# Four-head softmax tiles with a separate mask and maximum, re-timed planner costs, and a shorter warm-up in a one-core attention and feed-forward block

## The chip, the cores and the metric

The kernel runs on one core of a Trainium2 chip. The metric is device time in microseconds (us) of one execution; lower is better. The core has TensorE (PE, matrix products; its weight loads are PEld), VectorE (DVE), ScalarE (ACT), GpSimd (POOL) and SyncE (SP, which here only issues DMA transfers).

## What is computed

A layer of a transformer in float32, with the normalisation after each half. The input has 2 sequences of 1024 rows and 512 columns; attention has 16 heads of 32 columns and a causal mask; the feed-forward part uses the signs of its weights.

```python
qkv = jnp.einsum('bsd,ed->bse', x, w_qkv) + b_qkv          # 16 heads of 32
scores = jnp.einsum('bhqd,bhkd->bhqk', q, k) / math.sqrt(Hd)
scores = scores + causal[None, None]                       # -inf above the diagonal
out = jnp.einsum('bhqk,bhkd->bhqd', softmax(scores), v)
x = layernorm(x + jnp.einsum('bsd,ed->bse', out, w_out) + b_out)
hidden = relu(jnp.einsum('bsd,hd->bsh', x, sign(up_weight)) * up_scale)   # 2048 wide
out = jnp.einsum('bsh,dh->bsd', hidden, sign(down_weight)) * down_scale * output_scale
x = layernorm(x + out)
```

## The kernel before

The attention is done in eight chunks, two sequences by four groups of four heads. For each chunk the kernel makes queries, keys and values (`project`: products L554 for queries and keys, L591 for values), splits queries and keys into a rounded part and a remainder (`split`, `split_keys`), and lets SyncE copy them into the `stacks` tiles (`stack`), so that one pass of the float32r matmul gives a nearly exact score. Then it goes over row blocks of 128 queries, i = 0 to 7, each with (i + 1) x 128 keys.

A score tile ("sc", the program's `d`) is one of two PSUM buffers of 1024 columns. `grouped` puts four heads into a tile for i below 2, two for i below 4, else one. For a tile (`scores`): the score matmuls (L839; L820 for the first four row blocks of the first chunk, which use plain float32 and at most two heads), then one VectorE pass per head that adds the mask, negates and takes the minimum, which is minus the maximum (L857), then one ScalarE exponential per head with the row sum (L872), a reciprocal (L884), and a scaling per head on GpSimd (L890). TensorE transposes the result (L911, `transposes`), four 128x128 blocks to a PSUM bank, VectorE or ScalarE copies the bank to SBUF (L492 to L494), and TensorE multiplies with the values (L940, `values`). The output projection (L1005, `output`), the normalisation (`normalise`, which raises to the power -0.5 on GpSimd), the turned input (L1073), and the feed-forward products (L1122 and L1159) follow.

Nothing is issued in the order in which it is written. Each piece is a task with an engine, or a choice of engines, a cost, a due place and the tiles that it reads and writes. `Plan.schedule` runs a list scheduler over all tasks with these costs, chooses engines and buffers, and the instructions are issued in the order that comes out. The costs (`mm`, `dve`, `act`, `pool`, `copy` and the pairs given in braces) therefore do no work on the chip; they decide the order on every engine and which engine makes a copy. In a pair the first number is how long the engine is held, the second when the result is there.

The first stage (`first_half`) is ordered mostly by hand: 24 transposes of the identity (L710) on TensorE as a warm-up, then the first key and query weights on ScalarE's DMA queue, the first 256 columns of the transposed input in four pieces and the next 256 in one on SyncE's, then the products for these columns (L754) and their biases (L771 on VectorE for queries, L779 on ScalarE for keys). The bias vector `bqk` is loaded by GpSimd ahead of everything (L336). Five copies of one column (`hold`, L701) make later transfers wait for the first input piece.

Of the kernel before, what the change touches and what calls it, by code (L numbers as in the profile page):

```python
# [13 lines left out]
ALU = mybir.AluOpType  # L14
# [4 lines left out]
P = 128  # L19
# [257 lines left out]
def kernel(  # L277
# [55 lines left out]
    half = const.tile([P, 1], F32, tag="half", name="half")  # L333
    nc.gpsimd.memset(half, -0.5)
    bqk = const.tile([P, b_qkvP.shape[1]], F32, tag="bqk", name="bqk")
    nc.gpsimd.dma_start(bqk, b_qkvP)  # L336
    ups = const.tile([P, NFC], F32, tag="ups", name="ups")
    osc = const.tile([P, 1], F32, tag="osc", name="osc")
    bo = const.tile([P, D], F32, tag="bo", name="bo")
# [27 lines left out]
    def place_for(stack, name, n, kind=F32, side="left"):  # L367
# [24 lines left out]
        "v": views(a_v, (NQ, P)),  # L392
        "wout": views(a_wo, (NC, D)),
        "xb": views(a_xb, (D,)),
        "atT": views(a_at, (NC, P)),
        "nm": views(a_sm, (NU,))[:NSM],
        "sums": views(a_sm, (NU,), at=NSM * NU)[:NSM],
# [67 lines left out]


    def mm(n):
        return {"PE": (max(0.112, n / 2400 + 0.018),) * 2}

    def fp32(n):  # L470
        return {"PE": (n / 600 + 0.009,) * 2}
# [31 lines left out]
    def new(cls, after=(), blocks=1):  # L503
        t = plan.tile(cls, [y for c in after for y in all_of[c]], blocks)
        all_of[cls].append(t)
        return t

    def dma(place, dst, src, kb, reads=(), writes=(), updates=(), queue=DMA, label="dma", after=()):
        def fn(e):
            engine[e].dma_start(dst(), src())  # L510

        return plan.task(
            queue, fn, place, reads, writes, updates, size=kb, label=label, after=after
        )
# [190 lines left out]
    def first_half():  # L705

        warm = new("f")
        for k in range(24):
            plan.task(
                TURN, lambda _, k=k: nc.tensor.transpose(of(warm)[:, k % 4, :], ident, ident), -300,  # L710
                updates=[warm[0]], label="warm",
            )
        act_queue = {"ACT": (0.5, 0.5)}
        w = weights[0, 0] = new("w")
        for c, z in ((0, 1), (1, NC)):
            dma(
                -100,
                lambda c=c, z=z: of(w)[:, c:z, 1, :],
                lambda c=c, z=z: w_qkvT[c * P : z * P, D : D + P].rearrange(
                    "(c p) f -> p c f", p=P  # L720
                ),
                64 * (z - c),
                writes=[w[1, k] for k in range(c, z)],
                queue=act_queue,
            )
        xt = inputs[0] = new("xT")
        for t0, pieces in ((0, NC), (HB, 1)):
            for c in range(0, NC, NC // pieces):
                z = c + NC // pieces
                dma(  # L730
                    -100,
                    lambda c=c, z=z, t0=t0: of(xt)[:, c:z, t0 : t0 + HB],
                    lambda c=c, z=z, t0=t0: xT[c * P : z * P, t0 : t0 + HB].rearrange(
                        "(c p) t -> p c t", p=P
                    ),
                    128 * (z - c),
                    updates=[xt[k, t0] for k in range(c, z)],
                )
        load_w(0, 0, -95, [0], act_queue)
        hold(  # L740
            lambda: of(xt)[:, 0, 0:1], [xt[0, 0]],
            [lambda: of(w)[:, 0, 2, 0:1], *[lambda c=c: of(xt)[:, c, TB : TB + 1] for c in range(NC)]],
            [w[2], *[xt[c, TB] for c in range(NC)]],
        )
        load_w(0, 0, -90, [2])
        load_x(0, -80, [TB])
        v, kq = new("v"), new("pt", blocks=8)
        rows = lambda n: of(kq)[:, n * TB : (n + 1) * TB]
        for t0 in (0, HB):
            for n in (1, 0):  # L750
                ps = new("f")
                for c in range(NC):
                    def fn(_, c=c, n=n, t0=t0, ps=ps):
                        nc.tensor.matmul(  # L754
                            bank(ps)[:, :HB],
                            lhsT=of(w)[:, c, n, :],
                            rhs=of(xt)[:, c, t0 : t0 + HB],
                            start=(c == 0),
                            stop=(c == NC - 1),
                        )  # L760

                    plan.task(
                        fp32(HB), fn, -50, [xt[c, t0], w[n, c] if n else w[n]],
                        updates=[ps[0]], count=2, label="ps",
                    )
                bias = bqk[:, n * NC : n * NC + 1]
                dst = lambda n=n, t0=t0: rows(n)[:, t0 : t0 + HB]
                if n == 0:
                    plan.task(
                        dve(0.42),  # L770
                        lambda _, dst=dst, ps=ps, bias=bias: nc.vector.tensor_scalar(  # L771
                            dst(), bank(ps)[:, :HB], bias, scale, ALU.add, ALU.mult
                        ),
                        -50, [ps[0]], [kq[n, t0]], label="bias",
                    )
                else:
                    plan.task(
                        act(0.47),
                        lambda _, dst=dst, ps=ps, bias=bias: nc.scalar.activation(  # L779
                            dst(), bank(ps)[:, :HB], AF.Identity, bias=bias  # L780
                        ),
                        -50, [ps[0]], [kq[n, t0]], label="bias",
                    )
        values_of(0, 0, v, 0, lambda units=0: -1)
        plain[0, 0] = kq, v
# [25 lines left out]
    def scores(b, e, i, heads, at):  # L811
# [38 lines left out]
                        updates=[sc[0]], label="sc",  # L850
                    )

        for j in range(G):
            some = lambda j=j: of(sc)[:, j * W : j * W + N]
            plan.task(
                dve(0.17 + 1.046 * N / 1000),
                lambda _, j=j, some=some: nc.vector.tensor_tensor_reduce(  # L857
                    some(),
                    some(),
                    mask[:, S - N :],  # L860
                    scale=-1.0,
                    scalar=LARGEST,
                    op0=ALU.add,
                    op1=ALU.min,
                    accum_out=of(nm)[:, j : j + 1],
                ),
                at, [sc[0]], [sc[1, j], nm[j]], label="max",
            )
        for j in range(G):
            plan.task(  # L870
                {"ACT": (0.355 + 0.838 * N / 1000, 0.46 + 0.838 * N / 1000)},
                lambda _, j=j: nc.scalar.activation(  # L872
                    of(pr)[:, j * N : (j + 1) * N],
                    of(sc)[:, j * W : j * W + N],
                    AF.Exp,
                    bias=of(nm)[:, j : j + 1],
                    scale=-1.0,
                    accum_out=of(sums)[:, j : j + 1],
                ),
                at, [sc[1, j], nm[j]], [pr[j], sums[0]], label="exp",  # L880
            )
# [46 lines left out]
    def values(b, e, some, at):  # L928


        for i, _ in some:
            if (b, i) not in atT:
                atT[b, i] = new("atT")
        to, v = new("po"), (made.get((b, e)) or plain[b, e])[1]

        def fn(_):
            for n, (i, each) in enumerate(some):
                for k in range(i, -1, -1):
                    for u, pt, c in each[::-1]:
                        nc.tensor.matmul(  # L940
                            of(to)[ts(u, HD), n, :],
                            lhsT=of(v)[:, k, ts(u, HD)],
                            rhs=of(pt)[:, ts(c + k, P)],
                            start=(k == i),
                            stop=(k == 0),
                        )

        blocks = sum(i + 1 for i, _ in some)
        last = max(i for i, _ in some)
        plan.task(  # L950
            {"PE": (0.28 + 0.218 * blocks, 0.2 + 0.218 * blocks)}, fn, at,
            [v[t] for t in range(0, (last + 1) * P, TB)]
            + [pt[0] for _, each in some for _, pt, _ in each],
            updates=[to[0]], count=8 * blocks, label="po",
        )
        for n, (i, _) in enumerate(some):
            rows = atT[b, i]
            plan.task(
                dve(0.345),
                lambda _, n=n, rows=rows: nc.vector.tensor_scalar(  # L960
                    of(rows)[:, e, :],
                    of(to)[:, n, :],
                    bqk[:, 2 * NC + e : 2 * NC + e + 1],
                    None,
                    ALU.add,
                ),
                at - FAST, [to[0]], [rows[e]], label="at",
            )
# [59 lines left out]
    def normalise(b, at):  # L1028
# [7 lines left out]
            at, [m[0]], [m[1]], label="eps",  # L1036
        )
        plan.task(
            pool(1.2),
            lambda _: nc.gpsimd.tensor_tensor(  # L1040
                rs(), rs(), half.to_broadcast([P, NQ]), ALU.pow
            ),
# [298 lines left out]
```

## Time and profile before

| | us |
|---|---|
| median of three runs | 776.39 (776.19 to 776.39) |
| profiled execution | 775.87 |
| its span, first to last instruction | 774.1 |
| TensorE busy / weight loads | 756.1 / 574.9 |
| VectorE, ScalarE, GpSimd busy | 492.4, 368.9, 259.1 |
| attention part ends, feed-forward runs to the end | near 505 |

The span is what the trace covers; the execution's time has 1.8 us around it. In lines of the timeline the columns are start, duration, engine and line, operation, and in brackets how long the engine sat idle before it and what ended that. In stretches there is, for each engine, busy time and the number of instructions. In groups by shape, the numbers after the first bar are busy time in all and the mean duration in ns; after the second bar, the idle time before. A matmul in float32 is two instructions; the recorded durations of matmuls overlap, so the pitch from start to start is what TensorE is held for.

### The profile page before, as it was taken

The page shows a single profiled execution, that of the slowest core. Times are in us where ns is not written, and L with a number is a line of the kernel's source. Part 1 is how long each engine was busy: PE and PEld are TensorE (multiplying, and loading weights), DVE is VectorE, ACT ScalarE, POOL GpSimd, SP SyncE. Part 2 cuts the span into 40 slices and gives each one's busy share as a digit, 9 for nine tenths or more (in the row PEclk, how much of TensorE's full clock was granted, in tenths as well). Part 3 has the DMA queues.
Part 4 walks back from the last instruction along what each step waited for, and adds up shares of the span by engine and source line. Part 5 has one row for each costly group of instructions (what it writes and reads, how often), then busy time and mean ns, then how long its engine had stood idle before and what let it go on. Part 6 is the DMA issues. An engine that isn't in the chain of part 4 may idle for free.

```text
span 774.1 us, 15524 instructions
## 1 busy us (share of the span) xinstructions
PE 756.1 (98%) x5880; PEld 574.9 (74%) x5880; DVE 492.4 (64%) x1258; ACT 368.9 (48%) x823; POOL 259.1 (33%) x329
## 2 busy tenths in 40 slices
PE   8999999999999999999999999999999999999996
PEld 6668768768756776886876877657787787878884
DVE  2557878778766676877777878855337337335535
ACT  2337665666744455666666567744222222222210
POOL 3316445445535444544544545431002002002000
PEclk9999999999999999999999999999999999999999
DMA  5476436146453423523604614333001001000101
GB/s 163 106 175 148 135 83 140 40 100 155 130 110 83 96 69 85 111 67 68 152 1 95 139 56 137 137 109 109 1 0 55 1 0 55 1 0 1 55 0 54
DMA packets 38617, 62.35 MB, mean 81 GB/s; under 512 B 6032, under 2 KB 19344, under 8 KB 38544
## 3 DMA queue, kind: packets, MB, share of 16 engines
q1 hardware_dynamic: 37440, 60.85, 30.6%
q8 instruction: 46, 0.75, 0.4%
q10 hardware_dynamic: 1072, 0.52, 0.2%
q14 instruction: 27, 0.22, 0.1%
q0 software_dynamic: 32, 0.01, 0.0%
HBM read 24.66 MB, written 4.19 MB: 37 GB/s over the span
## 4 chain that ended last, share of the span: by engine, by line
PE 86%; DVE 9%; ACT 3%; issue 1%; POOL 1%; ACTq 0%; POOLq 0%; DVEq 0%
PE s L1122 14%; PE pd L1159 14%; PE s L911 13%; PE s L554 12%; PE d L839 9%; PE s L940 9%; PE s L1005 6%; PE s L591 6%; DVE d L857 3%; ACT probs L872 2%; DVE probsT L494 1%; PE s L754 1%; ACT probsT L492 1%; DVE small L1189 1%; PE s L1073 1%
## 5 line engine op out<-in xcount | busy, mean ns | idle before, releaser
L890 POOL TENSOR_SCALAR probs<-probs,small 128x128 f32<-128x128 f32 (+7 forms) x256 | 188.6, 748 | 249.6 <-DVE small L884 231.0
L872 ACT ACTIVATE probs<-d,small 128x128 f32<-128x128 f32 (+7 forms) x256 | 189.1, 748 | 61.6 <-DVE small L857 33.9
L857 DVE CUSTOM_DVE_ANT_0 d<-d,mask 128x128 f32<-128x128 f32 (+7 forms) x256 | 194.0, 765 | 31.5 <-PE d L839 19.9
L911 PE MATMUL s<-ident,probs 128*128 128x128 f32 x1152 | 164.4, 273 | 1.7 <-DVE probsT L494 0.8
L911 PEld LDWEIGHTS s<-ident,probs 128*128 128x128 f32 x1152 | 133.9, 141 | 32.8 <-issue 19.9
L492 ACT COPY probsT<-s 128x512 f32<-128x512 f32 (+3 forms) x184 | 90.9, 528 | 129.4 <-PE s L911 114.8
L1159 PE MATMUL pd<-stacks,hid 128*128 128x512 f32 x512 | 133.1, 399 | 0.5 <-DVE hid L1139 0.5
L1122 PE MATMUL s<-xt,stacks 128*128 128x512 f32 x512 | 132.7, 399 | 0.0
L1133 ACT ACTIVATE hf<-s,ups 128x512 f32<-128x512 f32 x64 | 44.0, 688 | 164.1 <-PE s L1122 162.4
L554 PE MATMUL s<-xT,wqkv 128*128 128x512 f32 x240 | 119.0, 599 | 2.1 <-ACT probsT L492 1.6
L839 PE MATMUL d<-stacks 128*128 128x512 f32 (+2 forms) x368 | 117.0, 416 | 1.1 <-ACT probs L872 0.4
L1159 PEld LDWEIGHTS pd<-stacks,hid 128*128 128x128 f32 x512 | 94.1, 188 | 24.2 <-DVE hid L1139 1.4
L1122 PEld LDWEIGHTS s<-xt,stacks 128*128 128x128 f32 x512 | 94.3, 188 | 23.4 <-issue 1.0
L494 DVE COPY probsT<-s 128x512 f32<-128x512 f32 (+3 forms) x161 | 91.1, 582 | 27.4 <-PE s L911 24.4
L1139 DVE CAST hid<-hf 128x512 fp32r<-128x512 f32 x64 | 27.3, 427 | 121.5 <-ACT hf L1133 121.4
L839 PEld LDWEIGHTS d<-stacks 128*128 128x128 f32 x368 | 58.7, 190 | 37.5 <-issue 20.4
L940 PEld LDWEIGHTS s<-probsT,v 128*32 128x32 f32 x2304 | 60.4, 110 | 20.4 <-ACT probs L872 7.6
L591 PE MATMUL s<-wqkv,xT 128*128 128x128 f32 x512 | 73.3, 275 | 0.0
L940 PE MATMUL s<-probsT,v 128*32 128x128 f32 x2304 | 71.6, 274 | 1.4 <-ACT probsT L492 1.0
L591 PEld LDWEIGHTS s<-wqkv,xT 128*128 128x128 f32 x512 | 67.2, 191 | 6.2 <-issue 4.8
L1005 PE MATMUL s<-wout,atT 128*128 128x512 f32 x128 | 63.7, 595 | 0.5 <-ACT probsT L492 0.5
L554 PEld LDWEIGHTS s<-xT,wqkv 128*128 128x128 f32 x240 | 39.2, 190 | 25.2 <-issue 20.6
(66 smaller groups left out, 496.1 us busy)
## 6 DMA issues: line engine op xcount, KB each, us to landing
stacks<-wqkv SPq DMA_DIRECT2D x224, 128.0 KB, 2.4
wqkv<-in_w_qkvT SPq DMA_DIRECT2D x22, 256.0 KB, 3.7
rows<-in_x SPq DMA_DIRECT2D x16, 256.0 KB, 2.7
raw<-in_up_wT SPq DMA_DIRECT2D x4, 1024.0 KB, 5.0
out<-atT SPq DMA_DIRECT2D x16, 256.0 KB, 2.0
xT<-in_xT SPq DMA_DIRECT2D x12, 256.0 KB, 5.5
stacks<-wqkv SPq DMA_DIRECT2D x48, 64.0 KB, 2.0
raw<-in_down_wT SPq DMA_DIRECT2D x2, 1024.0 KB, 5.5
```

The costliest lines, as they stand in the source:

```text
L494: nc.vector.tensor_copy(dst, src)
L554: nc.tensor.matmul(of(ps).rearrange("p a b -> p (a b)"), lhsT=of(w)[:, c, n, :], rhs=of(xt)[:, c, t0 : t0 + TB], start=(c == 0), stop=(c = ...
L591: nc.tensor.matmul(of(ps)[:, t, :], lhsT=of(xt)[:, c, t0 + t * P : t0 + (t + 1) * P], rhs=of(w)[:, c, 2, :], start=(c == 0), stop=(c == NC ...
L839: nc.tensor.matmul(of(sc)[:, j * W + k0 : j * W + k1], lhsT=of(st)[:, 0, u, ts(i, P)], rhs=of(st)[:, 1, u, k0:k1], start=True, stop=True,)
L857: lambda _, j=j, some=some: nc.vector.tensor_tensor_reduce(some(), some(), mask[:, S - N :], scale=-1.0, scalar=LARGEST, op0=ALU.add, op1= ...
L872: lambda _, j=j: nc.scalar.activation(of(pr)[:, j * N : (j + 1) * N], of(sc)[:, j * W : j * W + N], AF.Exp, bias=of(nm)[:, j : j + 1], sca ...
L890: lambda _, j=j: nc.gpsimd.tensor_scalar(of(pr)[:, j * N : (j + 1) * N], of(pr)[:, j * N : (j + 1) * N], of(sums)[:, j : j + 1], 1.0, ALU. ...
L911: lambda _, k=k, c=c, tp=tp: nc.tensor.transpose(of(tp)[:, k, :], of(pr)[:, c], ident),
L940: nc.tensor.matmul(of(to)[ts(u, HD), n, :], lhsT=of(v)[:, k, ts(u, HD)], rhs=of(pt)[:, ts(c + k, P)], start=(k == i), stop=(k == 0),)
L1005: lambda _, c=c: nc.tensor.matmul(bank(py), lhsT=of(a)[:, c, :], rhs=of(wout)[:, c, :], start=(c == 0), stop=(c == NC - 1),),
L1122: lambda _, f=f, c=c, n=n, pu=pu: nc.tensor.matmul(of(pu), lhsT=of(up)[:, f // TPB, c, ts(f % TPB, P)], rhs=of(xt)[:, n, c, :], start=(c = ...
L1159: lambda _, f=f, t=t, n=n, h=h: nc.tensor.matmul(of(pds[t]), lhsT=of(h)[:, ts(t, P)], rhs=of(dn)[:, f // 4, f % 4, :], start=(f == 0 and n ...
```

## The change

There are five edits.

1. Tiles of four heads: the four fused passes become one add of the mask's last 128 columns to the last 128 columns of each head, and one reduction that gives the negated maximum of all four heads. The exponential then runs with scale +1, not -1. Tiles of one and two heads stay as they are.
2. Costs of the plan: the least cost of a float32r matmul 0.062 (was 0.112), the exponential held 0.25 + 0.852 N/1000 (was 0.355 + 0.838 N/1000), the value group 0.15 + 0.218 per block (was 0.28), the power on GpSimd 1.7 (was 1.2), and costs for the two new operations.
3. The bias vector is no longer loaded by GpSimd; it is a tile of the plan, loaded on ScalarE's queue between the first key weights and the rest of them. The two first biases now depend on it in the plan.
4. The first input columns come in three pieces (one, one and two blocks of rows), not four.
5. Twelve warm-up transposes, not 24.

```diff
-    nc.gpsimd.dma_start(bqk, b_qkvP)
...
-        return {"PE": (max(0.112, n / 2400 + 0.018),) * 2}
+        return {"PE": (max(0.062, n / 2400 + 0.018),) * 2}
...
-        for k in range(24):
+        for k in range(12):
...
+            if c == 0:
+                dma(-100, lambda: bqk, lambda: b_qkvP, 8, writes=[biases[0]], queue=act_queue)
...
-        for t0, pieces in ((0, NC), (HB, 1)):
-            for c in range(0, NC, NC // pieces):
-                z = c + NC // pieces
+        for t0, c, z in ((0, 0, 1), (0, 1, 2), (0, 2, NC), (HB, 0, NC)):
...
-                        -50, [ps[0]], [kq[n, t0]], label="bias",
+                        -50, [ps[0], biases[0]], [kq[n, t0]], label="bias",
...
+        sign = 1.0 if G == 4 else -1.0
+        if G == 4:
+            sc3 = lambda: of(sc).rearrange("p (g w) -> p g w", g=G)[:, :, :N]
+            plan.task(
+                dve(0.163 + 0.134 * G),
+                lambda _: nc.vector.tensor_tensor(
+                    sc3()[:, :, N - P :],
+                    sc3()[:, :, N - P :],
+                    mask[:, None, S - P :].to_broadcast([P, G, P]),
+                    ALU.add,
+                ),
+                at, [sc[0]], [sc[1, j] for j in range(G)], label="mask",
+            )
+            plan.task(
+                dve(0.15 + 1.046 * N * G / 1000),
+                lambda _: nc.vector.tensor_reduce(of(nm)[:, :G], sc3(), AX.X, ALU.max, negate=True),
+                at, [sc[1, j] for j in range(G)], [nm[j] for j in range(G)], label="max",
+            )
...
-                {"ACT": (0.355 + 0.838 * N / 1000, 0.46 + 0.838 * N / 1000)},
+                {"ACT": (0.25 + 0.852 * N / 1000, 0.37 + 0.852 * N / 1000)},
...
-                    scale=-1.0,
+                    scale=sign,
...
-            {"PE": (0.28 + 0.218 * blocks, 0.2 + 0.218 * blocks)}, fn, at,
+            {"PE": (0.15 + 0.218 * blocks, 0.21 + 0.218 * blocks)}, fn, at,
...
-            pool(1.2),
+            pool(1.7),
```

## The prediction

> **What bounds the kernel now.** I read the page's busy times first, then the busy time by stretch, then the timeline of the first 25 us, then the waits of TensorE's weight loads, then the groups by shape. The page and the stretches:
>
> ```profile
> PE 756.1 (98%) x5880; PEld 574.9 (74%) x5880; DVE 492.4 (64%) x1258; ACT 368.9 (48%) x823; POOL 259.1 (33%) x329
> 0.00:10.00 10.00, 7.79 (x38) 7.46 (x39) 0.40 (x5) 1.28 (x1) 2.62 (x11) 1.00 0.84 254
> ...
> 750.00:775.00 25.00, 16.36 (x71) 12.84 (x69) 12.95 (x28) 2.55 (x6) 1.50 (x1) 0.93 0.11 42
> ```
>
> TensorE is the bound. It lacks 774.1 - 756.1 = 18.0 us: 2.2 before its first instruction, 24.1 - 16.4 = 7.7 after its last, and 8.1 in between. So work off TensorE is worth nothing unless TensorE waits for it, and three things can move the time: when real matmuls start, how the new order makes TensorE wait, and the tail. The start, from the timeline:
>
> ```profile
> 2.21 5.08 PE L710 MATMUL s<-ident 128*128 128x128 f32 x24 [2.21 <-POOL ident masks.py:199]
> ...
> 7.13 3.62 PE L754 MATMUL s<-xT,wqkv 128*128 128x256 f32 x16
> 8.02 1.28 ACT L779 ACT_TABLE_LOAD   x1 [8.02 <-DMA bqk<-in_b_qkvP]
> 10.35 0.47 ACT L779 ACTIVATE probsT<-s,bqk 128x256 f32<-128x256 f32 x1 [1.05 <-PE s L754]
> 10.79 0.48 DVE L771 TENSOR_SCALAR probsT<-s,bqk 128x256 f32<-128x256 f32 x1 [6.90 <-PE s L754]
> ...
> 11.42 0.50 PE L820 MATMUL d<-probsT 32*128 32x128 f32 x8 [0.67 <-DVE probsT L771]
> ```
>
> The 24 warm-up transposes fill TensorE from 2.21 to 7.13, one every 212 ns. The 16 instructions of the first key and query products follow, one every 216 ns. The first scores wait 0.67 us for the query bias on VectorE. The key bias waits for its product, not for the bias vector (landed at 8.02).
>
> **What the skill says.** The Trainium skill, "TensorE: Matmul & The Clock Gate", Part 1 (The HAM clock gate), says that TensorE runs at half rate until it has been busy for about 3.4 us. The trace agrees: a warm-up transpose takes 212 ns from start to start, while eight later ones (L911 at 149.58) take 1.03 us less one 0.27 us tail, 109 ns each. The same page (Engine queue depths) says that VectorE and ScalarE are strictly first in, first out, so a late head holds up what is behind; the 0.67 us wait above is of that kind. "DMA: Bandwidth & Descriptors", SWDGE vs HWDGE vs iDMA, says that transfers issued from ScalarE and SyncE run on the same DMA engines and have faster setup than GpSimd's. Here GpSimd's 6 KB bias took 5.5 us to land, ScalarE's 64 KB took 2.9. The first half is not contradicted: the DMA engines are 0.84 busy in the first 10 us.
>
> **The change, part by part.**
>
> *Start.* Twelve warm-ups go: 12 x 0.212 = 2.54 us of TensorE filler. The real gain ends where the data is. In the trace the first input block (issued 0.73, 2.7 us to land) is there at 3.4 and the first key weights (0.72 + 2.9) at 3.6. The rest of the key weights were issued at about 1.2 and landed 4.1 later, at 5.3; the last of the four input blocks (2.1 + 4.8) at 6.9, the query weights (1.65 + 4.9) at 6.6. New: ScalarE issues four transfers at 0.48 us each (1.43 us for three now), the bias second, so the key and query weights start 0.48 later: about 5.8 and 7.1. Input blocks 2 and 3 become one transfer of the same bytes; I put it between the old 5.7 (block 2) and 6.9 (block 3), at 6.7. The order of the changed program also puts all of the key product ahead of the query product, where now they alternate. So: transposes to 2.21 + 12 x 0.212 = 4.75; key block 0 at half rate, 2 x 0.43, to 5.6; block 1 from 5.8 to 6.65; blocks 2 and 3 from 6.7, 4 x 0.216, to 7.6; query 8 x 0.216, to 9.3. Now the query product ends at 10.75. Gain 1.4 us. Key bias and its table load come off the path altogether; the query bias still costs its wait. Bounds: 2.5 (all warm-ups count) and 0 (the clock wakes a window later and eight instructions take 0.43 instead of 0.216, which costs 1.7).
>
> What hangs on it moves too. GpSimd does the key cast (L616) now at 14.99 after three normalisations, in the new order after two; SyncE's chain of 48 stack transfers begins right behind it at 15.61, one per 0.63 us, and supplies the first scores of L839 at 50.23. It should begin some 2 us earlier, the scores that need it come some 2.3 us earlier: no new wait there, within 0.5 us. GpSimd loses a 0.77 us issue at 2.43, where it idles until 13.96; ScalarE gains a 0.48 us issue, where it idles until 8.02. SyncE issues one transfer less. All nothing.
>
> *Four heads per step.* These are the first two row blocks of seven of the eight chunks, 14 tiles (the reciprocal on 128x4 counts 14). From the groups by shape:
>
> ```profile
> L857 DVE CUSTOM_DVE_ANT_0 d<-d,mask 128x1024 f32<-128x1024 f32 x32 | 38.9, 1232 | 1.3 <-PE d L839 0.9
> ...
> L857 DVE CUSTOM_DVE_ANT_0 d<-d,mask 128x256 f32<-128x256 f32 x32 | 13.8, 431 | 7.6 <-ACT probs L872 3.7 <-PE d L839 2.7 <-PE d L820 0.8
> ...
> L857 DVE CUSTOM_DVE_ANT_0 d<-d,mask 128x128 f32<-128x128 f32 x32 | 9.5, 300 | 3.0 <-PE d L839 1.5 <-PE d L820 0.8
> ...
> L1020 DVE BATCH_NORM_STATS2 small<-x 128x6 f32<-128x512 f32 x8 | 5.5, 692 | 0.1
> L1016 DVE TENSOR_TENSOR x<-s,rows 128x512 f32<-128x512 f32 x8 | 5.5, 690 | 4.7 <-PE s L1005 4.7
> ```
>
> Now four passes and their four accumulator reads start 0.43 us apart at 128 columns and 0.52 at 256 (timeline, 12.06 to 18.46): 1.72 and 2.08 us a tile. New: one add over 4x128 (like L1016, 0.69) and one reduction over 512 (like L1020, 0.69) or 1024 elements (like the 1232 ns pass): 1.38 and 1.92. VectorE saves 7 x (0.34 + 0.16) = 3.5 of 492.4 us. Nothing of it is on the path by itself. Against it, the first exponential waits for the whole pair, not for one pass: 1.38 - 0.43 = 0.95 and 1.92 - 0.52 = 1.4 us later, and the score buffer is released after four exponentials (0.36 and 0.47 each, 0.2 for the last read): at 3.0 and 4.0 us instead of 2.3 and 2.7. There are two such buffers. Pricing the matmuls in the changed program's order by their pitch, TensorE has at least 4.5 us of other work before it needs one back after such a tile, mostly 4.5 to 6.9. Cover holds with 0.5 to 2.9 us to spare for a queue on VectorE. I take 0; bounds -1 (VectorE's relief) to +5 (14 x 0.35).
>
> *The plan's costs.* They do no work; they change the order. On TensorE the order stays alike over most of the attention part and is the same from about 505 us on, the tail included. Where it differs I look at the wait that matters:
>
> ```profile
> PEld d L839 <- ACT probs L872: 14.9, 39, 1.0
> PEld s L940 <- ACT probs L872: 7.6, 10, 0.8
> ```
>
> These are loads of score and value matmuls held until a score buffer or a copied block is free; most are hidden behind running matmuls. In the new order the first 640-column tile's buffer is wanted again after one short value group and two matmuls, 1.2 us, where its maximum, exponential (0.83 + 0.14 + 0.81) and semaphores need about 2.1: +0.9 us, once, near 48 us. In the old order that gap is 2.3 or more. The last long value group of the attention part follows its last transposes by 0.2 us, not 0.65, with a copy of 0.69 between: +0.4. On the other side, the exponential is now planned at its real pitch (0.25 + 0.852 x 0.256 = 0.47 us at 256 columns, the 0.47 of the timeline; the old plan had 0.57), and a 128-column matmul at 0.07 instead of 0.112: copies move three blocks from VectorE to ScalarE. I credit 0.8 of the 8.1 us idle in between; bounds -3 to +4. Sum: +0.5.
>
> **Sum.** -1.4 + 0 + 0.5 = -0.9 us on the profiled execution of 775.87 (its span 774.1 and 1.8 around it). The median of the runs, 776.39, is 0.5 above it; on that, 775.4.
>
> **Rivals.** A measurement can tell 0.2%, 1.55 us, from no change.
> - *Start gain kept, partly given back in the new order*: 775.4, within the bound. For it: a gain that the arrival of data limits, two places that lose by count. I give it 0.35.
> - *The clock wakes late*: with fewer warm-ups and a wait for data, the first products run at half rate, -1.4 + 1.7 + 0.5 = +0.8: 777.2. Against it: TensorE has next to no pause between 2.2 and 6.7. 0.08.
> - *The order gains as well*: an exponential planned right keeps ScalarE's queue true, and TensorE loses 1.5 us less of its 8.1: -1.4 - 1.5 = -2.9, 773.5. For it: VectorE is 75 to 80% busy in the attention stretches (38 of 50 us), so its relief may count. 0.38.
> - *Slower: the score buffers*. The pair of the four-head tiles holds a buffer 0.7 and 1.3 us longer. Where VectorE has a copy of 0.69 us ahead of the pair, release moves to 4.7, past the 4.5 us of cover; it decides from there. At 0.35 us for each of 14 tiles, 4.9 - 1.4 + 0.5 = +4.0: 780.4; half as many tiles, 777.9. Against it: the plan knows this hold. 0.19.
>
> **How the numbers follow.** Faster 0.38; within 0.2% 0.35 + 0.08 = 0.43; slower 0.19. The time is the likeliest case's, 775.4; that case alone spans 774.3 to 776.8. The range takes in most of the faster and about half of the slower case: 772.6 to 778.6.
>
> **What would show it.** Right: the last of the first 16 product instructions starts near 9.1, not 10.5; the first stack transfer near 13.5; L839's first scores near 48, with a wait of about 1 us behind them; VectorE some 3 to 4 us less busy; the part after 505 us unchanged but shifted. Wrong: first products at 430 ns each until 9 or 10 (late clock); a new wait of score matmuls on the exponentials of 128x128 and 128x256 tiles (buffers); idle time of TensorE in between well below 8 or above 10 us (the order).

## The result, and the profile after

| | before | after |
|---|---|---|
| median of six runs each, us | 775.91 | 772.87 |
| lowest to highest | 775.13 to 776.39 | 772.42 to 773.81 |
| ratio, with its 95% interval | | 0.9963 (0.9950 to 0.9976) |
| span of the profiled execution | 774.1 | 771.3 |
| first scores (L820 / L821) start | 11.42 | 13.14 |
| first feed-forward product (L1122 / L1143) starts | 520.77 | 518.04 |

The changed kernel is faster by 0.37%, 3.0 us, more than the 0.2% that can be told from no change. The forecast was 775.4 with a range from 772.6 to 778.6, its likeliest case no change beyond 0.2%: the range holds the time just above its low end, and what came is the case to which it gave 0.38, by other steps than its own. That the range holds is luck: two terms were wrong by 3.1 and by 4.95 us, with opposite signs.

Three stretches take the span apart. To the first scores the new kernel is 13.14 - 11.42 = 1.7 us slower. From there to the first feed-forward product it needs 504.9 us, not 509.35: 4.45 us faster. From there to the end it is 253.3 us in both. So the start lost where a gain was forecast, and the attention part gained where a small loss was.

The middle stretch, before and after, in the columns of the stretches (length, then busy time and instructions of TensorE, its weight loads, VectorE, ScalarE and GpSimd; the share of the clock, the DMA engines' busy share and GB/s):

```profile
11.42:520.77 509.35, 502.45 (x4767) 371.66 (x4767) 372.94 (x1015) 306.70 (x726) 238.38 (x305) 1.00 0.42 104
```

```profile
13.14:518.04 504.90, 500.13 (x4766) 372.37 (x4767) 373.69 (x929) 306.74 (x726) 238.07 (x305) 1.00 0.42 104
```

TensorE's idle time falls from 6.9 to 4.8 us, so 2.1 of the 4.45 us come out of idle time. The other 2.3 come out of its busy time, with the same matmuls: so recorded busy time is not all work, and what shortens in it no view shows.

The page of the changed kernel, busy times; then its timeline at the start (start, duration, engine, what, and the idle time before with what ended it):

```profile
PE 754.0 (98%) x5868; PEld 574.7 (75%) x5868; DVE 494.2 (64%) x1174; ACT 368.9 (48%) x823; POOL 257.7 (33%) x328
```

```profile
2.19 2.82 PE L710 MATMUL s<-ident 128*128 128x128 f32 x12 [2.19 <-POOL ident masks.py:199]
...
4.11 1.28 ACT L780 ACT_TABLE_LOAD   x1 [4.11 <-DMA bqk<-in_b_qkvP]
...
4.81 1.06 PE L755 MATMUL s<-xT,wqkv 128*128 128x256 f32 x2
...
7.33 5.14 PE L755 MATMUL s<-xT,wqkv 128*128 128x256 f32 x14 [1.45 <-DMA wqkv<-in_w_qkvT]
10.26 0.47 ACT L780 ACTIVATE probsT<-s,bqk 128x256 f32<-128x256 f32 x1 [4.87 <-PE s L755]
12.51 0.48 DVE L772 TENSOR_SCALAR probsT<-s,bqk 128x256 f32<-128x256 f32 x1 [8.67 <-PE s L755]
...
13.14 0.49 PE L821 MATMUL d<-probsT 32*128 32x128 f32 x4 [0.67 <-DVE probsT L772]
```

The transposes now end near 4.8 and the first key block runs there, as forecast. Then TensorE stands for 1.45 us until the rest of the key weights is there, and the fourteen instructions from 7.33 take 5.14 us, 0.37 each, where the kernel before needed 0.216: they start 0.43 us apart up to 10.9, at half rate, and 0.216 apart from there. The bias is early (table load at 4.11), the weights are late. The DMA issues of the first 2.6 us say so; the columns are the transfer, the issuing queue, count, size, and us from issue to landing. Before:

```profile
wqkv<-in_w_qkvT ACTq DMA_DIRECT2D x1, 256.0 KB, 4.9
wqkv<-in_w_qkvT ACTq DMA_DIRECT2D x1, 192.0 KB, 4.1
```

After:

```profile
wqkv<-in_w_qkvT ACTq DMA_DIRECT2D x1, 256.0 KB, 7.1
wqkv<-in_w_qkvT ACTq DMA_DIRECT2D x1, 192.0 KB, 5.6
wqkv<-in_w_qkvT ACTq DMA_DIRECT2D x1, 64.0 KB, 2.9
bqk<-in_b_qkvP ACTq DMA_DIRECT2D x1, 6.0 KB, 2.9
```

The same two weight transfers, behind the 6 KB of the bias, need 2.2 and 1.5 us longer from their own issue.

In the attention part, these are the waits of the weight loads in the changed kernel, and TensorE's own (us in all, times, longest):

```profile
PEld d L840 <- ACT probs L893: 22.6, 58, 0.9
...
PEld s L961 <- ACT probs L893: 7.6, 10, 0.8
```

```profile
PE d L840 <- ACT probs L893: 2.6, 4, 0.7
PE s L710 <- POOL ident masks.py:199: 2.2, 1, 2.2
PE s L932 <- DVE probsT L494: 1.7, 2, 0.9
PE s L755 <- DMA wqkv<-in_w_qkvT: 1.5, 1, 1.5
```

The wait for score buffers has grown, from 14.9 us to 22.6, while the part became faster: this sum alone doesn't explain the gain. Where it lies shows in one chunk. The timeline of before, near the group of 64 value matmuls of the second chunk:

```profile
145.71 1.12 PE L554 MATMUL s<-xT,wqkv 128*128 128x512 f32 x2 [0.53 <-ACT probsT L492]
...
146.76 1.69 PEld L940 LDWEIGHTS s<-probsT,v 128*32 128x32 f32 x64 [0.76 <-ACT probs L872]
...
152.46 0.30 PEld L839 LDWEIGHTS d<-stacks 128*128 128x128 f32 x2 [0.95 <-ACT probs L872]
```

and of after, in the same chunk:

```profile
150.79 1.28 DVE L494 COPY probsT<-s 128x512 f32<-128x512 f32 x2
...
152.38 0.68 DVE L878 CUSTOM_DVE_ANT_0 d<-d,mask 128x512 f32<-128x512 f32 x1
...
155.44 0.30 PEld L840 LDWEIGHTS d<-stacks 128*128 128x128 f32 x2 [0.94 <-ACT probs L893]
155.44 0.56 PE L840 MATMUL d<-stacks 128*128 128x512 f32 x2 [0.71 <-ACT probs L893]
```

The product that waited 0.53 us for a copy behind exponentials no longer waits; in exchange two copies now stand ahead of a maximum on VectorE (150.79, then 152.38), and the score buffer that it releases comes 0.71 us late. The gain is the sum of such differences, chunk after chunk. TensorE is 1.7 us behind the kernel before at the first scores, 0.3 ahead at the last value product of the third chunk, 2.1 at that of the fifth and 2.7 at the first feed-forward product; no single wait carries it.

### The profile page after: what moved, and what is told of

It is laid out like the page before. It is cut to its first block, busy times and chain, and to the rows that moved or that the text cites. A ratio compares the mean times of both kernels' runs of the same rounds, so it can differ in the third digit from the quotient of the medians.

```text
span 771.3 us, 15421 instructions
## 1 busy us (share of the span) xinstructions
PE 754.0 (98%) x5868; PEld 574.7 (75%) x5868; DVE 494.2 (64%) x1174; ACT 368.9 (48%) x823; POOL 257.7 (33%) x328
## 4 chain that ended last, share of the span: by engine, by line
PE 91%; DVE 5%; ACT 2%; DMA 1%; issue 1%; ACTq 0%
PE s L932 15%; PE s L1143 14%; PE pd L1180 14%; PE s L554 13%; PE d L840 9%; PE s L961 8%; PE s L591 7%; PE s L1026 7%; DVE d L878 2%; ACT probs L893 2%; PE s L755 1%; PE s L1094 1%; DVE small L1210 1%; PE d L821 1%; DMA wqkv<-in_w_qkvT 1%; DVE atT L1194 1%
## 5 line engine op out<-in xcount | busy, mean ns | idle before, releaser
L878 DVE CUSTOM_DVE_ANT_0 d<-d,mask 128x384 f32<-128x384 f32 (+7 forms) x200 | 173.5, 875 | 20.2 <-PE d L840 16.5
L932 PE MATMUL s<-ident,probs 128*128 128x128 f32 x1152 | 160.9, 273 | 1.8 <-DVE probsT L494 1.7
L492 ACT COPY probsT<-s 128x512 f32<-128x512 f32 (+3 forms) x187 | 95.5, 539 | 130.5 <-PE s L932 120.2
L1143 PE MATMUL s<-xt,stacks 128*128 128x512 f32 x512 | 132.7, 399 | 0.0
L840 PE MATMUL d<-stacks 128*128 128x512 f32 (+2 forms) x368 | 116.1, 414 | 2.9 <-ACT probs L893 2.6
L1143 PEld LDWEIGHTS s<-xt,stacks 128*128 128x128 f32 x512 | 94.3, 188 | 23.4 <-issue 1.0
L494 DVE COPY probsT<-s 128x512 f32<-128x512 f32 (+3 forms) x158 | 87.8, 565 | 26.6 <-PE s L932 22.9
L840 PEld LDWEIGHTS d<-stacks 128*128 128x128 f32 x368 | 58.8, 189 | 42.7 <-ACT probs L893 22.6
L591 PE MATMUL s<-wqkv,xT 128*128 128x128 f32 x512 | 76.1, 275 | 0.0
L591 PEld LDWEIGHTS s<-wqkv,xT 128*128 128x128 f32 x512 | 69.0, 191 | 7.1 <-issue 5.5
```

Of the source, the lines that this page charges most:

```text
L492: nc.scalar.copy(dst, src)
L591: nc.tensor.matmul(of(ps)[:, t, :], lhsT=of(xt)[:, c, t0 + t * P : t0 + (t + 1) * P], rhs=of(w)[:, c, 2, :], start=(c == 0), stop=(c == NC ...
L840: nc.tensor.matmul(of(sc)[:, j * W + k0 : j * W + k1], lhsT=of(st)[:, 0, u, ts(i, P)], rhs=of(st)[:, 1, u, k0:k1], start=True, stop=True,)
L878: lambda _, j=j, some=some: nc.vector.tensor_tensor_reduce(some(), some(), mask[:, S - N :], scale=-1.0, scalar=LARGEST, op0=ALU.add, op1= ...
L932: lambda _, k=k, c=c, tp=tp: nc.tensor.transpose(of(tp)[:, k, :], of(pr)[:, c], ident),
L1143: lambda _, f=f, c=c, n=n, pu=pu: nc.tensor.matmul(of(pu), lhsT=of(up)[:, f // TPB, c, ts(f % TPB, P)], rhs=of(xt)[:, n, c, :], start=(c = ...
```

## The experiments

Two theories were set against each other. *Order*: the attention part gains because all tasks are put in another order, and the pair of operations itself is worth nothing. *Operation*: the pair relieves VectorE. For the start: *ring*, the bias ahead of the weights in ScalarE's DMA ring holds them up; against it, that twelve transposes are too few, or that landing doesn't matter. Each median stands beside the runs of before that it shared a chip with.

### The start

**Bias behind the key weights.** All engines keep the order of the changed kernel, only ScalarE's second and third transfer change places.

```diff
-            if c == 0:
+            if c == 1:
                 dma(-100, lambda: bqk, lambda: b_qkvP, 8, writes=[biases[0]], queue=act_queue)
```

> The changed kernel with the bias vector put behind the rest of the key weights on ScalarE's queue, not ahead of them; the order on all engines is else the same. Theory A (the 48-byte packets of the bias hold up the key weights behind them, TensorE pauses, and the clock wakes late): the rest of the key weights lands near 5.5 us instead of 7.2, TensorE hardly pauses, the clock is full near 7, the first scores start near 10.5 instead of 13.1, and the whole is 2 to 2.7 us below the changed kernel, about 770.4. Rival B (the weights are late because the input pieces take the DMA engines): weights still at about 7, time 772.9.

Measured: 772.07 us (before 775.80; ratio 0.9949, 0.9937 to 0.9962). The key weights land 4.2 us after their issue again, and the first products no longer wait:

```profile
4.81 3.18 PE L755 MATMUL s<-xT,wqkv 128*128 128x256 f32 x8
...
8.79 1.99 PE L755 MATMUL s<-xT,wqkv 128*128 128x256 f32 x8 [0.80 <-DMA wqkv<-in_w_qkvT]
...
11.45 0.49 PE L821 MATMUL d<-probsT 32*128 32x128 f32 x4 [0.67 <-DVE probsT L772]
```

The delay has moved one place on: now the query weights, which follow the bias, take 6.6 us and hold TensorE for 0.80. First scores at 11.45, not at the forecast 10.5, and the time fell by 0.8 us, not by 2 to 2.7. Even that is not told apart: the intervals of the two ratios overlap (0.9937 to 0.9962, 0.9950 to 0.9976). In the profile the ring theory is right on what delays what; it was wrong on how much is left once the key weights are free.

**24 transposes in the changed order.**

```diff
-                TURN, lambda _, k=k: nc.tensor.transpose(of(warm)[:, k % 4, :], ident, ident), -300,
+                TURN, lambda _, k=k: [nc.tensor.transpose(of(warm)[:, m % 4, :], ident, ident)
+                                      for m in (2 * k, 2 * k + 1)], -300,
```

> The changed kernel with 24 warm-up transposes again, two for each of the twelve tasks of the plan, so that the order stays the same. Theory A (pause and late clock cost the start): the key weights still land near 7.2 but the clock is full by 7, so the products run at 0.216 us each and the query weights (9.2) are the next limit; first scores near 11.6, the whole 1.3 to 1.7 us below the changed kernel, about 771.3. Rival B (only the landing matters, the clock wakes at a time of its own): 772.9.

Measured: 772.53 (before 775.80; 0.9959, 0.9945 to 0.9972). The first scores start at 11.92, 1.2 us ahead of the changed kernel's profile, because the products start 0.216 us apart from 8.1 on, not from 10.9; yet the medians differ by 0.3 only, within what single executions of the changed kernel differ by (772.42 to 773.81). The rival, no difference, is closer on the time.

**The start alone**, on the kernel before (bias on ScalarE's queue, three pieces, twelve transposes):

> The kernel before with the three edits of the start alone (bias on ScalarE's queue, three pieces, twelve warm-up transposes). Theory A (this start loses): first scores near 13.1 instead of 11.4, and 0.8 to 1.7 us slower than before, 776.6 to 777.5. Rival B (later stages absorb it): 775.8.

Measured: 777.85 (before 776.39; 1.0023, 1.0015 to 1.0031): slower, a little beyond theory A's range. Its profile has waits of the same kind, but the full rate from the second product instruction on:

```profile
4.82 0.68 PE L755 MATMUL s<-xT,wqkv 128*128 128x256 f32 x2
6.85 1.53 PE L755 MATMUL s<-xT,wqkv 128*128 128x256 f32 x6 [1.35 <-DMA wqkv<-in_w_qkvT]
9.24 1.99 PE L755 MATMUL s<-xT,wqkv 128*128 128x256 f32 x8 [0.86 <-DMA wqkv<-in_w_qkvT]
11.90 0.38 PE L821 MATMUL d<-probsT 32*128 32x128 f32 x2 [0.67 <-DVE probsT L772]
```

At 11.90, against 13.14 with the same code at half rate. So the moment of the full rate differs between executions, which made about 1.2 us here. The start before is not fixed either: in the seven profiles with that start (before and the six runs that keep it) the first scores come between 10.59 and 11.62, so single profiles of two starts tell differences of a microsecond only with care. Of the 1.3 us by which this profile's span is longer than before's, 0.5 are there at the first scores. Most of the rest comes within the first chunk, whose order the edits of the start change too; from the second chunk on the lag stays at 1.2. The median's loss is therefore not the late weights' alone.

**Bias by GpSimd, twelve transposes and three pieces kept:**

```diff
+    nc.gpsimd.dma_start(bqk, b_qkvP)
...
-            if c == 0:
-                dma(-100, lambda: bqk, lambda: b_qkvP, 8, writes=[biases[0]], queue=act_queue)
```

> The changed kernel with the bias vector loaded by GpSimd as before; twelve transposes and three pieces stay. Theory A (only the bias in ScalarE's ring spoils the start, the rest of it gains what was forecast): key weights near 5.2, query weights near 6.6, no pause, first scores near 10 and the time near 770.3, below both the changed kernel and the one with the old start (771.5). Rival B (twelve transposes are too few for the clock anyway): products at half rate until 8 or later, scores at 11 to 13, time 771.5 to 773.

Measured: 771.33 (before 776.39; 0.9951, 0.9932 to 0.9969). The seven executions spread from 770.34 to 775.94, and the ratio's interval overlaps that of the changed kernel: the profile shows the mended start, the time doesn't tell it apart. The weights land 4.0 and 5.1 us after issue, and the sixteen product instructions run from 4.82 to 10.2 with one pause of about 0.3 us, at 6.83. The first scores wait for the query bias on VectorE, which waits for the last product:

```profile
4.82 5.37 PE L752 MATMUL s<-xT,wqkv 128*128 128x256 f32 x16
...
9.83 0.47 ACT L777 ACTIVATE probsT<-s,bqk 128x256 f32<-128x256 f32 x1
10.23 0.48 DVE L769 TENSOR_SCALAR probsT<-s,bqk 128x256 f32<-128x256 f32 x1 [6.28 <-PE s L752]
...
10.86 0.49 PE L818 MATMUL d<-probsT 32*128 32x128 f32 x4 [0.67 <-DVE probsT L769]
```

The key bias is done at 10.30, ahead of the query bias at 10.71, so the bias vector is no limit here. The scores come at 10.86 and not near 10 because the products start 0.43 us apart up to 7.8, close to what rival B named. The busy time of the stretch from 3 to 6 us shows the ring at work in the last two numbers, the DMA engines' busy share and GB/s. (The share of the clock ahead of them stays 1.00 also where the products run at half rate; at the start only the pitch tells.) Before, after, bias behind the key weights, and bias by GpSimd, in this order:

```profile
3.00:6.00 3.00, 3.00 (x16) 3.00 (x15) 0.40 (x5) 0.00 (x0) 0.20 (x1) 1.00 1.01 292
```

```profile
3.00:6.00 3.00, 2.87 (x12) 2.15 (x10) 0.40 (x5) 1.28 (x1) 0.00 (x0) 1.00 0.78 205
```

```profile
3.00:6.00 3.00, 3.00 (x13) 2.74 (x12) 0.40 (x5) 0.00 (x0) 0.00 (x0) 1.00 0.87 260
```

```profile
3.00:6.00 3.00, 3.00 (x13) 2.82 (x12) 0.40 (x5) 0.00 (x0) 0.20 (x1) 1.00 0.99 301
```

With the bias ahead of the key weights the 16 DMA engines are not full: 205 GB/s, against 260 with it behind them and 292 and 301 with GpSimd loading it. From 3 to 4 us, ScalarE's queue alone (q10, told by its bytes; packets, MB, share of the 16 engines' time), before and after:

```profile
q10 hardware_dynamic: 233, 0.11, 38.7%
```

```profile
q10 hardware_dynamic: 120, 0.02, 12.6%
```

So the small packets don't fill the engines; the queue moves a fifth of the bytes in a third of the engines' time. The transfers behind the bias start late, they do not share a full pipe. What holds the ring up between the packets no run tells.

### The attention part

**Pair and new costs with the old start.**

> The pair for four-head tiles and the new costs of the plan, with the start of the kernel before (24 transposes, bias by GpSimd, four pieces). Theory A (the attention part gained some 4.4 us by order and pair, the start lost 1.7): 771.5, 4.4 below before. Rival B (the attention part gains because its start is displaced against SyncE's transfers): most of the gain goes, 775.

Measured: 771.49 (before 775.80; 0.9943, 0.9930 to 0.9955), 4.3 us below before: the size forecast. The gain is the attention part's own and does not hang on the new start.

**Four fused passes in the changed order.** `passes((0, 1))` and `passes((2, 3))` issue the old instruction for these heads where the add and the reduction stood, and the exponential has scale -1 again:

```diff
-                lambda _: nc.vector.tensor_tensor(
...
+                lambda _: passes((0, 1)),
...
-                lambda _: nc.vector.tensor_reduce(of(nm)[:, :G], sc3(), AX.X, ALU.max, negate=True),
+                lambda _: passes((2, 3)),
```

> The changed kernel in its own order, but each four-head tile again with four fused mask-and-maximum passes in the place of the pair. Theory A (the gain is the order, not the operation): within 0.6 us of the changed kernel, 772.3 to 773.5. Rival B (the pair relieves VectorE's queue or stops the accumulator reads): most of the attention gain goes, 776.

Measured: 773.38 (before 775.80; 0.9968, 0.9956 to 0.9979), 0.5 above the changed kernel: the operations are hardly worth anything.

**New costs alone** (the four changed figures in the plan, nothing else):

> The kernel before with the changed costs of the plan alone (matmul floor, exponential, value group, power). Theory A (the attention gain of 4.3 us comes from the order that these costs give): 771.5 to 772.5. Rival B (costs and pair work only together, or the pair's own durations in the plan change the order): 774 to 776.

Measured: 771.21 (before 776.39; 0.9939, 0.9927 to 0.9950): 5.2 us faster with the same work, only scheduled otherwise. The schedule is more than the order: the page counts 834 instructions on ScalarE, not 823, and 11 fewer on VectorE, so 11 copies changed the engine. "Order" below has that in it. No run takes the two apart; the changed kernel's gain of 4.45 us came with as many instructions on ScalarE as before (823).

**The pair alone** (its own two costs with it, all other costs and the start as before):

> The kernel before with the pair for four-head tiles alone, its own two costs with it, the other costs as before. Theory A: within 1 us of before, 775 to 776.5. Rival B (the pair carries the gain): 772.

Measured: 767.69 (before 776.39; 0.9892, 0.9880 to 0.9905): 8.7 us faster, the opposite of what theory A expected and 4.3 us more than rival B did. The next two take order and operation apart.

**The order of the pair-alone kernel with four fused passes** (the diff above, applied to that kernel):

> The order of the run with the pair alone (767.7), but with four fused passes of the kernel before in the place of each pair; no operation differs from the kernel before, only the order does. Theory A (the order that the pair's tasks give is worth the 8.7 us, the operations are not): 767 to 769. Rival B (the pair's shorter time on VectorE is what gains): 774 to 776.

**The order of before with the pair**, issued where the first of the four passes stood:

```diff
-                lambda _, j=j, some=some: nc.vector.tensor_tensor_reduce(
+                lambda _, j=j, some=some: pair(j) if G == 4 else nc.vector.tensor_tensor_reduce(
```

> The order of the kernel before on every engine, with the pair for four-head tiles in the place of the first of the four passes. Theory A (operations alone are worth little): within 1.5 us of before, 775 to 777. Rival B (the pair gains by itself): 768 to 771.

| | order of before | order of the pair-alone kernel |
|---|---|---|
| four fused passes | 776.39 | 767.97 (0.9892, 0.9877 to 0.9907) |
| pair | 776.03 (0.9999, 0.9991 to 1.0008) | 767.69 |

This settles it. The operations are worth nothing that can be told (0.4 and 0.3 us by the medians, both within the intervals); the order, with the engine of nine copies in it, 8.4 us. The pair gained only because two tasks with other costs make the scheduler put everything else elsewhere. These two waits of the weight loads say the same: with the pair in the order of before they are before's to the digit,

```profile
PEld d L839 <- ACT probs L883: 14.9, 39, 1.0
PEld s L951 <- ACT probs L883: 7.6, 10, 0.8
```

and with the fused passes in the other order both are less:

```profile
PEld d L839 <- ACT probs L893: 13.0, 42, 0.8
...
PEld s L961 <- ACT probs L893: 2.4, 4, 0.8
```

**The exponential's cost.** The pair, the old start and all new costs but one:

```diff
-                {"ACT": (0.25 + 0.852 * N / 1000, 0.37 + 0.852 * N / 1000)},
+                {"ACT": (0.355 + 0.838 * N / 1000, 0.46 + 0.838 * N / 1000)},
```

> The pair with the old start and all the new costs but the exponential's, which is planned as before at 0.355 + 0.838 N/1000. Theory A (the new, shorter cost of the exponential packs the score tiles tighter and loses 3.8 us of what the pair's order gains): 767 to 769. Rival B (each set of costs gives an order of its own and none of them is the reason): 770 to 775, with no relation to that cost.

Measured: 766.62 (before 776.39; 0.9869, 0.9854 to 0.9884), the fastest median here, 1.3% below before, near theory A's 767 to 769 and outside rival B's range. It differs from the kernel with the pair, the old start and all new costs by this one line: 9.8 us below the before of its chip, where that one is 4.3 below its own. The cost that fits the trace (0.47 us from one exponential to the next at 256 columns) gives the worse order, the one that is 0.1 us too long the better. Its waits:

```profile
PEld d L839 <- ACT probs L892: 6.9, 21, 0.7
```

6.9 us for score buffers, against 19.8 with the fitted cost (old start), 22.6 in the changed kernel, and 13.0 in the pair-alone kernel, which has the longer cost too. A reading, not shown: the longer cost makes the plan think that a score buffer comes free later, so it puts more matmuls between two uses, and the real release is then seldom late. Against a general rule stands that the kernel before has the long cost too and is the slowest of them, and that the fitted costs alone gained 5.2 us; each set of costs gives an order of its own.

**An attempt at the best of both**: the pair with the old costs, twelve transposes, three pieces, and the bias last on ScalarE's queue.

```diff
-            if c == 0:
-                dma(-100, lambda: bqk, lambda: b_qkvP, 8, writes=[biases[0]], queue=act_queue)
...
         load_w(0, 0, -95, [0], act_queue)
+        dma(-94, lambda: bqk, lambda: b_qkvP, 8, writes=[biases[0]], queue=act_queue)
```

> The pair alone with the old costs, and the start with twelve transposes, three pieces and the bias vector last on ScalarE's queue, behind the query weights. Theory A (the bias must not stand ahead of weights; the order of the pair-alone run survives over most of the program): key weights near 5.2, query weights near 6.7, bias near 7.3, first scores at 9.8 to 10.6, time 766.5 to 767.5. Rival B (the order changes enough to lose its gain): 769 to 772.

Measured: 770.01 (before 776.39; 0.9916, 0.9901 to 0.9931). The first scores start 0.3 us ahead of before's profile, which is within the 10.59 to 11.62 that the old start itself shows. The key weights hold TensorE for 0.84 us, and the scores then wait for the query bias behind the products. The bias lands late, at 8.84, but the key bias is done at 10.61, ahead of the query bias at 10.94:

```profile
7.56 2.86 PE L754 MATMUL s<-xT,wqkv 128*128 128x256 f32 x12 [0.84 <-DMA wqkv<-in_w_qkvT]
8.84 1.28 ACT L779 ACT_TABLE_LOAD   x1 [8.84 <-DMA bqk<-in_b_qkvP]
...
10.46 0.48 DVE L771 TENSOR_SCALAR probsT<-s,bqk 128x256 f32<-128x256 f32 x1 [6.54 <-PE s L754]
...
11.09 0.49 PE L820 MATMUL d<-probsT 32*128 32x128 f32 x4 [0.67 <-DVE probsT L771]
```

The order is alike but not the same as in the pair-alone kernel: the two profiles are level at 25 us, and this one is 1.7 behind at 65. Rival B had it.

## Why the prediction was right or wrong, point by point

- *TensorE is the bound, and only start, order and tail count*: right. The four-way table above moves the time by 8.4 us without touching any work, and the part from the first feed-forward product on is equal in both kernels, as forecast. But the 8.1 us of idle time were taken for all that an order can win; see the order below.
- *Start, -1.4 us*: wrong in sign, +1.7. The step that failed is "the key and query weights start 0.48 later: about 5.8 and 7.1". They did start 0.48 later, but landed at 7.2 and 9.2; an issue slot was charged for the bias, the time for which it holds up what is behind it in the ring was not. The late clock, given 0.08, showed in the profile of the changed kernel as well and did about 1.2 us of the damage there; "next to no pause between 2.2 and 6.7" rested on the same landing times. The sum was also short on the rate: four instructions were priced at 0.43 us, where even with GpSimd loading the bias six took that long, and the products ended at 10.2, not at 9.3. The delay of the clock with which the prediction reckoned is not a fixed one here: the pitch halves under 3 us after the first transpose in the profile of the start alone, and about 9 us after it in the changed kernel. That the key bias and its table load come off the path was right. The 0.67 us before the first scores are no matter of queues served in order, as the prediction had it: VectorE sat idle for 6.90 us ahead of the query bias, and the wait is this bias's own 0.48 us and its hand-over.
- *What hangs on the start*: nothing shows that stack transfers stopped the first scores of L840. They came 0.7 us later than before (50.93), not 2.3 earlier, behind first scores that came 1.7 later.
- *The pair, 0*: right, by the four-way table and the fused passes in the changed order. The sizes were right too:

```profile
L860 DVE TENSOR_TENSOR d<-d,mask 128x512 f32<-128x512 f32 x14 | 9.8, 699 | 2.3 <-PE d L840 2.3
L870 DVE TENSOR_REDUCE small<-d 128x4 f32<-128x1024 f32 x7 | 8.5, 1219 | 0.2
...
L870 DVE TENSOR_REDUCE small<-d 128x4 f32<-128x512 f32 x7 | 4.8, 681 | 0.0
```

  0.70 and 0.68 or 1.22 us, for 0.69 and 0.69 or 1.23. But "VectorE some 3 to 4 us less busy" was wrong: 494.2, not 492.4. The pair saves next to nothing: in the changed order VectorE is busy 494.0 us with the four passes and 494.2 with the pair, in the pair-alone order 487.7 and 487.4. The reading was at fault: the passes of a four-head tile on 128 columns stand 0.40 us apart (136.48, 136.88, 137.27 and 137.66 in the pair-alone order), not 0.43, and the last of a tile was charged for a whole step, though the next instruction can start before its read ends. The slower rival, buffers held too long by the pair, is ruled out: the pair in the order of before took 776.03, and the 22.6 us of waits for score buffers in the changed order are there with the four passes too.
- *The order, +0.5 with bounds of -3 and +4*: the term that was mis-sized, and the one that decided. It was -4.45, outside its bounds. The first place that was named came: TensorE waits 0.46 us at 53.41 for a score buffer (0.9 was forecast). Near the second, transposes wait 0.89 us for a copy at 494.67, while the value group right behind them, at 495.01, waits for nothing (0.4 was forecast). But two places out of dozens were counted, those that stand out in an order; what recurs from chunk to chunk was not. And the bound came from idle time, of which the order took 2.1 us in the middle stretch; 2.3 more came out of time recorded as busy. The credit of 0.8 "for an exponential planned right" had the wrong reason: with the other costs new, that cost loses 5.5 us, each kernel taken against the before of its chip. "The same from about 505 us on" holds for TensorE from 515 on.
- *The cases*: the time lies in the range and near the faster rival's 773.5. That rival's path, the start's 1.4 and 1.5 more, was not the one taken. The start's 1.4 with the order's 4.45 would have been some 770, below the range: it holds because the start failed too.

## What to carry to other kernels

Where a list scheduler writes the order, changing any task's cost or number reshuffles everything: compare an edit in a frozen order (emit the old instructions where the new tasks stand) before crediting it, and give the order itself bounds as wide as the waits it may move, here 9 us of 776, and wider than TensorE's idle time. A cost that fits the trace need not be the cost that gives the best order; try the neighbours on the chip. A tiny transfer put ahead of large ones in a DMA ring can cost more than its issue slot, so let the first weights go first, and look at when they land.

## What the runs showed of the hardware that was not expected

- 6 KB in rows of 48 bytes, one place ahead in ScalarE's ring, lengthened the transfer behind it from 4.1 to 5.6 us and the next from 4.9 to 7.1, and left the DMA engines at 205 instead of 292 GB/s from 3 to 6 us. The packets of ScalarE's queue took 12.6% of the engines' time from 3 to 4 us, so the small packets' own time is not what fills it.
- With equal code at the start, TensorE's first two product instructions took 0.68 us in one profiled execution and 1.06 in another, and the scores came at 11.90 and 13.14. In the six profiles with twelve transposes the products reach their full pitch between 4.8 and 10.9 us: the moment at which the clock wakes differs between executions, so a start should be judged by more than one profile.
- With the same matmuls, another order took 2.3 us out of TensorE's recorded busy time (502.45 to 500.13) and 2.1 out of its idle time: idle time is no bound on what an order can win.
